# Layer 3's first steps issued between the steps that follow the recurrent part's last scan

## The chip, the cores and the metric

The kernel runs on one core of one Trainium2 chip. The metric is device time of one execution in microseconds (us). A core has a matrix engine (TensorE, PE in the profile, with its weight loads as PEld), a vector engine (VectorE, DVE), a scalar engine (ScalarE, ACT), a general engine (GpSimd, POOL) and a synchronisation engine (SyncE, SP), which here only issues loads and stores. Each engine works through its own list of instructions in the order in which they were written into it; engines wait for each other by semaphores. Matrix products land in PSUM (8 banks, a tile of 128 x 512 float32 fills one), everything else lives in SBUF.

## The reference, cut to what matters

Four layers follow each other on an activation x of shape (4, 512, 512) in float32, with a context tensor of the same shape.

```
# layer 0: grouped-query cross attention of x on the context, then layer norm
# layers 1 and 2: an RWKV block; x is its only link to the layer before
def step(s, inp):                     # one time step, for all batches and heads
    k_l, v_l, w_l, r_l = inp
    a = k_l[..., :, None] * v_l[..., None, :]
    out = einsum('bhs,bhst->bht', r_l, faaaa * a + s)
    return a + w_l[..., None] * s, out
_, outs = scan(step, s0, (k, v, w, r))
y = group_norm(outs) * gn_w + gn_b
x = x + (y * g) @ Wo.T                # "outputs"
xc = layer_norm(x)
xk2, xr2 = xc + shift(xc) * fmaa_k, xc + shift(xc) * fmaa_r
x = x + sigmoid(xr2 @ fWr.T) * (square(relu(xk2 @ fWk.T)) @ fWv.T)   # "channels"
# layer 3: queries from x, keys and values from [context, x], a mask over the context
q = x @ q_w + q_b
k, v = split(concat([ctx, x]) @ kv_w + kv_b)
attn = softmax(where(mask, q k^T / 32, -inf))        # 16 heads of 32, 1024 keys
o = (attn v) @ out_w + out_b + x
out = gelu(rmsnorm(o) @ mlp_w1 + b1) @ mlp_w2 + b2 + x
```

Batches do not mix anywhere: layer 3 on batch 0 needs only batch 0 of layer 2's result.

## The kernel before, in words

The residual x lies in SBUF for the whole run (`xn[b][lt]`, 16 tiles of 128 x 512). Four 8 KB slots per partition (`wpool`, tag `w`) hold whatever 512 x 512 weight is in use.

Layer 0 runs first (to about 730 us). Layers 1 and 2 are one function, `recurrent` (L455): its 16 units are (layer, batch, half of 256 positions), in this order. A global counter `g` runs through 8 scan steps per unit; `end` is 128. At each `g`, `summed` (L881), `begun` (L833 to L844), `scan` (L862, L867) and `repeated` are called, and then the dictionary `steps` says which parts of the other generators are due, in four phases EARLY, SOON, MID, LATE. These are `mixes` (the projections ahead of the scan), `outputs` (group norm, gate, output product; from step 9 of its unit) and `channels` (the feed-forward part; from step 19 to step 27 of its unit). So the last scan, at `g` = 127, is followed by 28 more values of `g` in which there is no scan left, but

* at g = 128 to 131 the end of the channels of unit 13 (products fk, fr, fv at L73 from g = 128, 129 and 130),
* at 129 to 135 the outputs of unit 15: mean, square, variance, a power on POOL (L929), a broadcast product pbc, the scaling, and the product with Wo,
* at 131 to 139 the channels of unit 14,
* at 139 to 147 the channels of unit 15, which need the outputs of unit 15.

Layer 3 is the function `layer3` (L1087). It opens its pools, loads its constants (L1100 to L1110), and for batch 0 loads the context and the mask (`begin`, L1117 to L1126), turns x by 16 transposes into `xT` (L1131, L1132) and makes query, keys and values of a first group of four heads (`prep`, L1143 to L1159). Then a loop over steps `i` starts, 8 of them (NB) for each of the 16 (batch, head group) pairs. At step `i` it calls `least` for the present group (four score products `psc`, L1175, into four PSUM tiles, and four DVE instructions L1189 that keep the row's smallest value, which is the largest score since the query is negated), one piece of the next group's `prep`, and, for the group before, `spread` (L1208), `turned` (L1175 pst, L1220), `weights` and `values`. In the first 8 steps there is no group before, so only `least` and `prep` run.

The order of instructions on PE, DVE, ACT and POOL is the order of the source (`manual_schedule`). SP's queue, which issues the loads, is laid out by the compiler's planner instead: it sends a load when, by the planner's clock, its buffer is free. SP issues in order, and a load whose buffer is still in use holds up those behind it. The loads with accumulation (`added`, L584) are issued from POOL.

Pools are stacks of memory: a pool that opens where another has closed gets its space, and a tile of it waits until the last user of the tiles that lay there is done. Before, all tiles of the recurrent part lie in `rm`, `rs`, `rpv` (4 banks), `rpy` (1 bank) and `rpp` (3 banks), and these close after g = 155; layer 3's pools open on the same space:

```
with tc.manual_schedule(engines={E.PE, E.DVE, E.Activation, E.Pool}):   # second block
    layer3()
```

Of the kernel before, what the change touches and what calls it, by code (L numbers as in the profile page):

```python
# [30 lines left out]
def tile_xattn_rwkv_perceiver(ctx: ExitStack, tc: tile.TileContext, t: dict, out: bass.AP):  # L31
# [422 lines left out]

    def recurrent(lp, ep):  # L455
        NI = 4
# [6 lines left out]

        mp = sp = pvr = pyp = W = A = None

# [89 lines left out]
        def scaled(tag, tiles, nm, rstd):  # L555
            if mp:
                z = mp.tile([P, NT, C], F32, tag=tag, name="z", bufs=BUFS[tag])
            else:
                z = wpool.tile([P, 2, NT, C], F32, tag="w", name="z0")[:, 0]
            for i, x in enumerate(tiles):  # L560
                nc.scalar.activation(
                    z[:, i], x, AF.Identity, bias=nm[:, i : i + 1], scale=rstd[:, i : i + 1]
                )
            return z
# [28 lines left out]
        def mixes(q):  # L593
# [83 lines left out]
            def product(x):  # L677
                dst = d[x] = mp.tile(full, F32, tag="o_" + x, name="o_" + x, bufs=1 if x == "v" else 2)
                dst4 = dst.rearrange("p i (o m) -> p i o m", o=2)
# [117 lines left out]
            yield 0, LATE  # L797
            y = d["y"] = mp.tile(full, F32, tag="y", name="y")
            nc.gpsimd.tensor_tensor(y, d["v"], al[:, None, :].to_broadcast(full), ALU.mult)
# [96 lines left out]
        def outputs(q):  # L896
# [8 lines left out]
            mm(pm, [(gmean, y[:, i, :]) for i in range(NI)])  # L905
            mean = sp.tile([P, TS], F32, tag="mean", name="mean", bufs=1)
            nc.scalar.copy(mean, pm)
            yield 9, LATE
            nc.vector.tensor_tensor(y, y, mean[:, None, :].to_broadcast(full), ALU.subtract)
            yield 10, EARLY  # L910
            sq = mp.tile(full, F32, tag="cx", name="sq", bufs=BUFS["cx"])
            nc.scalar.activation(sq, y, AF.Square)
            yield 10, SOON
            var = psum_tile([P, NQ], "var")
            for i in range(NI):
                for a in range(4):
                    nc.tensor.matmul(
                        var[32 * a : 32 * a + 32],
                        gm32,
                        sq[:, i, NQ * a : NQ * a + NQ],  # L920
                        start=(i == 0),
                        stop=(i == NI - 1),
                        tile_position=(0, 32 * a),
                    )
            yield 10, LATE
            rstd = sp.tile([P, NQ], F32, tag="gn_rs", name="gn_rs")
            nc.vector.tensor_scalar(rstd, var, 1.0, 1e-5, ALU.mult, ALU.add)  # L927
# [8 lines left out]
            mm(pm, [(gself, rp)])  # L936
            bc = sp.tile([P, TS], F32, tag="mean", name="bc", bufs=1)
            nc.scalar.copy(bc, pm)
# [3 lines left out]

            yg = mp.tile(full, F32, tag="cx", name="yg", bufs=BUFS["cx"])
            for i in range(NI):
# [24 lines left out]
        def channels(q):  # L969
# [8 lines left out]
            yield 22, EARLY  # L978
            cur = mp.tile([P, KC, TS], F32, tag="xc", name="xc", bufs=1)
            turned(z, vec, cur, V_LN2W, V_LN2B)  # L980
            last = d["lastc"] = sp.tile([P, KC], F32, tag="lastc", name="lastc")
            nc.scalar.copy(last, cur[:, :, TS - 1])
            yield 22, MID
            sx = mp.tile([P, KC, TS], F32, tag="sxc", name="sxc", bufs=1)
            shift(sx, cur, stT[:, :, b, 0] if hf == 0 else st[q - 1]["lastc"])

            def shifted(name, i):
                dst = mp.tile([P, KC, TS], F32, tag="cx", name=name, bufs=BUFS["cx"])
                for k in range(KC):
                    nc.scalar.activation(dst[:, k], sx[:, k], AF.Copy, scale=vec[:, k, i : i + 1])  # L990
                added(dst, cur)
                return dst
# [6 lines left out]

            kk = mp.tile([P, KC, TS], F32, tag="cx", name="kk", bufs=BUFS["cx"])  # L1000
            fk = load_w(t[n + "fWk"], n + "fk")
# [52 lines left out]
        end = G * len(units)  # L1054
        with (
            tc.tile_pool(name="rm", bufs=2) as mp,
            tc.tile_pool(name="rs", bufs=2) as sp,
            tc.tile_pool(name="rpv", bufs=1, space=PSUM) as pvr,
            tc.tile_pool(name="rpy", bufs=1, space=PSUM) as pyp,
            tc.tile_pool(name="rpp", bufs=3, space=PSUM) as pp,  # L1060
        ):
            psum["p"] = pp, "p"


            W = [mp.tile([P, 8, TP + 1], F32, tag=f"W{i}", name=f"W{i}", bufs=1) for i in range(2)]
            A = mp.tile([P, 8, TP + 1], F32, tag="A", name="A", bufs=1)
            for z in (*W, A):
                nc.gpsimd.memset(z[:, :, 0:1], 0.0)
            for g in range(at[0], end + 28):
                if 0 < g <= end:  # L1070
                    summed(g - 1)
                if -1 <= g < end - 1:
                    begun(g + 1)
                if 0 <= g < end:
                    scan(g)
                if 0 < g < end - 2 and g % NI == NI - 2:
                    repeated(*place(g + 2)[:2])
                for ph in (EARLY, SOON, MID, LATE):
                    for q, gen in steps.pop((g, ph), ()):
                        at = next(gen, None)  # L1080
                        if at:
                            follow(q, at, gen)
                    if ph == MID and 0 < g <= end and g % NI == 0:
                        taken(g - 1)


    def layer3():  # L1087
# [3 lines left out]
        T2 = 2 * P  # L1091
        with (
            tc.tile_pool(name="l3c", bufs=1) as cp,
            tc.tile_pool(name="l3b", bufs=1) as bp,
            tc.tile_pool(name="l3s", bufs=2) as sp,
            tc.tile_pool(name="l3ps", bufs=7, space=PSUM) as ps_s,
            tc.tile_pool(name="l3po", bufs=1, space=PSUM) as ps_o,
        ):
            cols = cp.tile([P, KC, 3], F32, name="cols3")
# [13 lines left out]
            def begin(b):  # L1113
# [3 lines left out]
                nc.sync.dma_start(cT, t["ctxT"][:, b * L : (b + 1) * L].rearrange("(k p) n -> p k n", p=P))  # L1117
                mi = sp.tile([P, L], I32, tag="sc", name="mi")
                nc.sync.dma_start(mi, t["mask3"][b : b + 1, :].to_broadcast([P, L]))
# [59 lines left out]
            def least(u, lt, a):  # L1179
# [3 lines left out]
                if (lt, a) == (0, 0):  # L1183
                    d["mx", m] = sp.tile([P, 2, LT, NR], F32, tag="mx", name="mx", bufs=2)
                mx = d["mx", m]
                ps = row_scores(d["q", m][:, lt * P : (lt + 1) * P], d["k", m][:, a, :], "psc")
                for r in range(NR):
                    sc = sp.tile([P, L], F32, tag="sc", name="sc", bufs=2)
                    nc.vector.tensor_tensor_reduce(  # L1189
# [10 lines left out]
            def spread(u):  # L1200

                b, m = u
                d = st[b]
                mb = d["mb"] = sp.tile([P, NR, L], F32, tag="mb", name="mb", bufs=1)
                for r in range(NR):
# [57 lines left out]
            def inverted(u):  # L1263
                d = st[u[0]]
                rs = d["rs"] = sp.tile([P, L], F32, tag="sc", name="rs")
                nc.vector.reciprocal(rs, d["pn"])
# [8 lines left out]
            def finish(b):  # L1275
# [5 lines left out]
                for lt in range(LT):  # L1281
# [5 lines left out]
                    nc.vector.tensor_tensor(ao, ao, x, ALU.add)  # L1287
                    sq = sp.tile([P, C], F32, tag="sc", name="sq")
                    ss = sp.tile([P, 1], F32, tag="ss", name="ss")
# [6 lines left out]
                for h in range(L // T2):  # L1296
                    nT = bp.tile([P, KC, T2], F32, tag="nT", name="nT", bufs=2)
                    for k in range(0, KC, 2):
# [16 lines left out]
                for h in range(L // T2):  # L1315
                    nT = nTs[h]
                    for j in range(4):
                        m1 = load_w(t["L3_W1"][:, j * C : (j + 1) * C], f"l3_m1_{j}")
                        hT = bp.tile([P, KC, T2], F32, tag="hT", name="hT", bufs=2)
                        for m in range(0, KC, 2):  # L1320
# [38 lines left out]
            LAG = 2  # L1359
            for _ in chain(begin(0), prep(0, 0)):  # L1360
                pass
            early = rest = iter(())
            left = 0
            for i in range(NU + NB + LAG):
                n, s = divmod(i, NB)
                u, old = [units[j] if 0 <= j < len(units) else None for j in (n, n - 1)]
                if u and s == 0:
# [17 lines left out]
                elif piece(rest):  # L1385
                    left -= 1
                if old:
                    if s == 0:
# [20 lines left out]
    E = mybir.EngineType  # L1409
    with (  # L1410
        tc.manual_schedule(engines={E.PE, E.DVE, E.Activation, E.Pool}),
        tc.tile_pool(name="rl", bufs=1) as lp,
        tc.tile_pool(name="rt", bufs=2) as ep,
    ):
        ahead = recurrent(lp, ep)
        layer0(ahead, ep)
        for _ in ahead:
            pass
    with tc.manual_schedule(engines={E.PE, E.DVE, E.Activation, E.Pool}):
        layer3()  # L1420

# [63 lines left out]
```

## Time and profile before

| | |
|---|---|
| median of 3 runs | 3794.02 us (3792.13 to 3795.58) |
| profiled execution | 3798.02 us, its span 3796.2 us, granted TensorE clock 0.966 |
| busy share of the span | PE 94%, DVE 73%, ACT 44%, POOL 47% |

By stage, in us (cut at the first layer-1 product, the last scan, layer 3's first projection, and the first step of layer 3 that works on two groups):

| stage | length | PE busy | DVE busy | ACT busy | POOL busy | granted clock |
|---|---|---|---|---|---|---|
| layer 0, 0 to 730 | 730 | 708.5 | 543.5 | 481.9 | 500.7 | 0.98 |
| 730 to 2290, recurrent part with scans | 1560 | 1425.5 | 1354.2 | 673.0 | 699.8 | 0.96 |
| 2290 to 2426.6, what follows the last scan | 136.6 | 93.1 | 19.0 | 34.7 | 33.4 | 0.84 |
| 2426.6 to 2479.2, layer 3's first group alone | 52.6 | 52.5 | 23.8 | 4.1 | 0 | 0.92 |
| 2479.2 to the end | 1317.0 | 1290.8 | 819.5 | 474.4 | 537.0 | 0.98 |

A row of the timeline begins with its start and its length in us, then the engine, the line, the operation, and the output and input by the program's names; what stands in brackets is how long the engine was idle before it and who released it. Matrix products are pipelined: the time from one row's start to the next row's start is what one costs in a stream, and it is a little less than the length shown.

### The profile page before, as it was taken

The page shows a single profiled execution, that of the slowest core. Times are in us where ns is not written, and L with a number is a line of the kernel's source. Part 1 is how long each engine was busy: PE and PEld are TensorE (multiplying, and loading weights), DVE is VectorE, ACT ScalarE, POOL GpSimd, SP SyncE. Part 2 cuts the span into 40 slices and gives each one's busy share as a digit, 9 for nine tenths or more (in the row PEclk, how much of TensorE's full clock was granted, in tenths as well). Part 3 has the DMA queues.
Part 4 walks back from the last instruction along what each step waited for, and adds up shares of the span by engine and source line. Part 5 has one row for each costly group of instructions (what it writes and reads, how often), then busy time and mean ns, then how long its engine had stood idle before and what let it go on. Part 6 is the DMA issues. An engine that isn't in the chain of part 4 may idle for free.

```text
span 3796.2 us, 52369 instructions
## 1 busy us (share of the span) xinstructions
PE 3570.5 (94%) x20544; PEld 1900.4 (50%) x20544; DVE 2759.9 (73%) x4665; ACT 1668.2 (44%) x2486; POOL 1771.0 (47%) x834
## 2 busy tenths in 40 slices
PE   9999999988899999999999977799999999999989
PEld 3333333455565666655655544444455445544446
DVE  6777777689988888888888882177866766667531
ACT  4777675533444444444444432133334434434421
POOL 4777876524544444444444443045533433344330
PEclk9999999989999999999999988899999999999999
DMA  4000000156676777777777764400022122121223
GB/s 151 24 12 23 12 9 20 40 141 141 146 171 165 170 188 177 170 173 179 163 171 167 169 156 111 111 28 19 15 76 83 56 70 95 56 73 34 95 95 122
DMA packets 188805, 386.66 MB, mean 102 GB/s; under 512 B 18128, under 2 KB 44880, under 8 KB 186512
## 3 DMA queue, kind: packets, MB, share of 16 engines
q1 hardware_dynamic: 150256, 251.72, 20.9%
q0 software_dynamic: 38304, 131.61, 18.7%
q8 instruction: 162, 2.65, 0.3%
q14 instruction: 83, 0.68, 0.1%
HBM read 247.50 MB, written 4.19 MB: 66 GB/s over the span
## 4 chain that ended last, share of the span: by engine, by line
PE 71%; DVE 13%; DMA 6%; issue 4%; POOL 3%; ACT 2%; SPq 0%; DVEq 0%; POOLq 0%; ACTq 0%
PE pm L73 9%; PE ph L73 6%; PE pv L73 6%; PE po L73 6%; DMA kv<-A 5%; PE psc L242 5%; PE pst L279 4%; PE pst L1175 4%; PE psc L1175 4%; PE pr L73 3%; PE pk L73 3%; PE po L304 3%; PE po L1241 3%; DVE ry L867 3%; DVE kv L862 2%
## 5 line engine op out<-in xcount | busy, mean ns | idle before, releaser
L1236 POOL TENSOR_TENSOR acc<-acc,aT 128x2048 f32<-128x2048 f32 x96 | 436.2, 4544 | 337.5 <-ACT aT L1231 220.0
L292 POOL TENSOR_TENSOR aT<-aT,nmT 128x1536 f32<-128x1536 f32 x124 | 428.7, 3461 | 205.5 <-ACT aT L290 182.2
L254 DVE CUSTOM_DVE_ANT_0 sc<-psc,nm 128x512 f32<-128x512 f32 x512 | 354.1, 692 | 147.2 <-PE psc L242 89.5
L1220 DVE TENSOR_TENSOR aT<-pst,mb 128x512 f32<-128x512 f32 x512 | 317.7, 683 | 166.0 <-PE pst L1175 166.0
L867 DVE TENSOR_TENSOR ry<-kv,o_r 128x1024 f32<-128x1024 f32 x256 | 347.4, 1398 | 3.5
L584 POOL DMA_DIRECT2D kv<-A x127 | 118.8, 936 | 381.4 <-DVE kv L839 378.3
L862 DVE TENSOR_TENSOR_SCAN kv<-W,kv 128x1032 f32<-128x1032 f32 x128 | 296.3, 2315 | 0.2 <-DMA kv<-A 0.2
L290 ACT COPY aT<-pst 128x512 f32<-128x512 f32 x372 | 196.5, 595 | 177.9 <-PE pst L279 177.4
L298 ACT ACTIVATE aT<-aT 128x2048 f32<-128x2048 f32 x128 | 246.7, 1929 | 5.4 <-POOL aT L292 4.6
L73 PE MATMUL ph<-nT,l_m 128*128 128x256 f32 x1024 | 238.1, 388 | 0.0
L73 PE MATMUL po<-l_m,hT 128*128 128x512 f32 x512 | 233.1, 602 | 0.0
L73 PEld LDWEIGHTS ph<-nT,l_m 128*128 128x128 f32 x1024 | 193.6, 193 | 64.1 <-issue 24.8
L833 DVE TENSOR_TENSOR A<-vr,o_k 128x1024 f32<-128x1024 f32 x128 | 155.7, 1217 | 87.9 <-DMA kv<-A 87.8
L279 PE MATMUL pst<-q,km 32*128 32x512 f32 x1024 | 206.5, 640 | 9.4 <-DVE mxs L254 5.8
L1234 POOL TENSOR_TENSOR acc<-aT 128x2048 f32<-128x2048 f32 x16 | 72.4, 4527 | 303.2 <-ACT aT L1229 303.2
L1189 DVE CUSTOM_DVE_ANT_0 sc<-psc,zeros,mx 128x512 f32<-128x512 f32 x256 | 176.6, 746 | 51.2 <-PE psc L1175 49.0
L1231 ACT ACTIVATE aT<-aT 128x2048 f32<-128x2048 f32 x64 | 122.3, 1911 | 191.8 <-DVE aT L1220 191.6
L1229 ACT ACTIVATE aT<-aT,mc 128x2048 f32<-128x2048 f32 x64 | 128.1, 2002 | 165.1 <-DVE aT L1220 158.9
L242 PE MATMUL psc<-km,q 32*128 32x512 f32 x1024 | 198.5, 651 | 0.8 <-ACT q L223 0.8
L929 POOL TENSOR_TENSOR gn_rs<-gn_rs,mhalf 128x64 f32<-128x64 f32 x16 | 186.4, 11648 | 23.1 <-DVE gn_rs L927 23.1
L881 PE MATMUL py<-ry,k 128*32 128x512 f32 x1024 | 159.6, 637 | 39.1 <-DVE ry L867 27.6
L1189 DVE CUSTOM_DVE_ANT_0 sc<-psc,nm 128x512 f32<-128x512 f32 x256 | 161.1, 686 | 39.2 <-PE psc L1175 39.2
(265 smaller groups left out, 7153.3 us busy)
## 6 DMA issues: line engine op xcount, KB each, us to landing
l_m<-in_L_W SPq DMA_DIRECT2D x64, 1024.0 KB, 5.1
kv<-A POOLq DMA_DIRECT2D x127, 516.0 KB, 7.4
L_wk<-in_L_Wk SPq DMA_DIRECT2D x16, 1024.0 KB, 8.0
L_wr<-in_L_Wr SPq DMA_DIRECT2D x16, 1024.0 KB, 7.7
L_wv<-in_L_Wv SPq DMA_DIRECT2D x16, 1024.0 KB, 5.9
L_wg<-in_L_Wg SPq DMA_DIRECT2D x16, 1024.0 KB, 8.0
L_wo<-in_L_Wo SPq DMA_DIRECT2D x64, 256.0 KB, 7.6
L_fk<-in_L_fWk SPq DMA_DIRECT2D x16, 1024.0 KB, 7.8
```

The source lines that it names most:

```text
L73: nc.tensor.matmul(ps, lhsT, rhs, start=(i == 0), stop=(i == len(pairs) - 1))
L242: nc.tensor.matmul(psc, d["q"][g][rs, lt * P : (lt + 1) * P], d["km"][rs, a, :], start=True, stop=True, tile_position=(32 * r, 0),)
L254: nc.vector.tensor_tensor_reduce(sc, ps[r], d["nm"][lt], 1.0, -3.0e38, ALU.add, ALU.max, mxs[:, a, lt, c : c + 1])
L279: nc.tensor.matmul(pst, d["km"][rs, a, s * P : (s + 1) * P], d["q2", a][rs, :], start=True, stop=True, tile_position=(32 * r, 0),)
L292: nc.gpsimd.tensor_tensor(w[:, n:, :], w[:, n:, :], nmT[:, None, :].to_broadcast([P, NR - n, L]), ALU.add)
L298: nc.scalar.activation(w, w, AF.Exp)
L862: nc.vector.tensor_tensor_scan(flat(kv), flat(W[g % 2]), flat(kv), 0.0, ALU.mult, ALU.add)
L867: nc.vector.tensor_tensor(y, kv[:, 4 * h : 4 * h + 4, None, :TP].to_broadcast([P, 4, 2, TP]), d["r"][:, i].rearrange("p (o m) -> p o m", o ...
L1175: nc.tensor.matmul(psc, lhsT[rs], rhs[rs], start=True, stop=True, tile_position=(32 * r, 0))
L1189: nc.vector.tensor_tensor_reduce(sc, ps[r], d["nm"][a], 1.0, mx[:, 0, lt, r : r + 1] if a else 3.0e38, ALU.add, ALU.min, mx[:, a, lt, r : ...
L1220: nc.vector.tensor_tensor(w[:, r, :], ps[r], d["mb"][:, r, :], ALU.subtract)
L1236: nc.gpsimd.tensor_tensor(d["acc", m], d["acc", m], w, ALU.add)
```

## The change

It does four things.

1. The recurrent part's pools are split. Tiles that are still used after the last scan (the gate `o_g`, `y`, everything with tag `cx`, `xc`, `sxc`, `mean`, `gn_rs`, `lastc`) move to new pools `rq` and `rt2`; they and the 3 banks of `rpp` are opened first. The rest (`rm`, `rs`, `rpv`, `rpy`) is opened on top and closed at g = 128. Names, sizes and numbers of buffers stay as they are (`sq` as a tile name becomes `y2`).
2. Layer 3's `cp` and `bp` are opened on the other end of SBUF, and a first PSUM pool of 5 banks (`l3pf`), where `rpv` and `rpy` were. The tiles that the first steps need (`mi`, `sc`, `mx`, `mb`, and with them `rs` and `sq` of tag `sc`) go to `bp`; `nT` and `hT` go from `bp` to `l3s`. `l3s`, the 7 banks of `l3ps` and the one of `l3po` are opened after the recurrent part's pools are closed.
3. `layer3` becomes a generator. It yields at each point where `begin` and `prep` yield (2 and 5 times) and after each of the first 8 steps `i` (8 times), then "closed". `recurrent` takes one such piece after the LATE phase of each g from 129 on, so the 15 pieces stand at g = 129 to 143, and the one that closes `l3pf` at 144. The pieces are: constants, loads of batch 0 and half of the transposes; the other half; q; k of the context; v of the context; k of x; v of x; then five times `least` with a piece of the next group's `prep` (q, k, v, k, v), and three times `least` alone.
4. There is one `manual_schedule` block instead of two.

```diff
-        with (
-            tc.tile_pool(name="rm", bufs=2) as mp,
-            tc.tile_pool(name="rs", bufs=2) as sp,
-            tc.tile_pool(name="rpv", bufs=1, space=PSUM) as pvr,
-            tc.tile_pool(name="rpy", bufs=1, space=PSUM) as pyp,
-            tc.tile_pool(name="rpp", bufs=3, space=PSUM) as pp,
-        ):
+        with ExitStack() as below, ExitStack() as above:
+            mq = below.enter_context(tc.tile_pool(name="rq", bufs=2))
+            sq = below.enter_context(tc.tile_pool(name="rt2", bufs=2))
+            pp = below.enter_context(tc.tile_pool(name="rpp", bufs=3, space=PSUM))
+            mp = above.enter_context(tc.tile_pool(name="rm", bufs=2))
+            sp = above.enter_context(tc.tile_pool(name="rs", bufs=2))
+            pvr = above.enter_context(tc.tile_pool(name="rpv", bufs=1, space=PSUM))
+            pyp = above.enter_context(tc.tile_pool(name="rpy", bufs=1, space=PSUM))
...
+                if g == end:
+                    above.close()
+                elif g > end:
+                    next(beside, None)
+            for _ in beside:
+                pass
...
     def layer3():
...
-            tc.tile_pool(name="l3c", bufs=1) as cp,
-            tc.tile_pool(name="l3b", bufs=1) as bp,
-            tc.tile_pool(name="l3s", bufs=2) as sp,
-            tc.tile_pool(name="l3ps", bufs=7, space=PSUM) as ps_s,
-            tc.tile_pool(name="l3po", bufs=1, space=PSUM) as ps_o,
+            cp = opened("l3c", 1, side="right")
+            bp = opened("l3b", 1, side="right")
+            first = ExitStack()
+            ps_s = first.enter_context(tc.tile_pool(name="l3pf", bufs=5, space=PSUM))
...
-            for _ in chain(begin(0), prep(0, 0)):
-                pass
+            yield from chain(begin(0), prep(0, 0))
...
             for i in range(NU + NB + LAG):
                 n, s = divmod(i, NB)
+                if i == NB:
+                    first.close()
+                    yield "closed"
+                    sp = opened("l3s", 2)
+                    ps_s = opened("l3ps", 7, space=PSUM)
+                    ps_o = opened("l3po", 1, space=PSUM)
...
+                if i < NB:
+                    yield
...
-        ahead = recurrent(lp, ep)
+        third = layer3()
+        ahead = recurrent(lp, ep, iter(third.__next__, "closed"))
         layer0(ahead, ep)
         for _ in ahead:
             pass
-    with tc.manual_schedule(engines={E.PE, E.DVE, E.Activation, E.Pool}):
-        layer3()
+        both.close()
+        for _ in third:
+            pass
```

## The prediction

> **What bounds the kernel now.** I read the stages first (busy time of each engine by window). Their columns are the window, its length, then busy time and instructions of PE, PEld, DVE, ACT and POOL, the granted clock, the DMA share and GB/s.
>
> ```profile
> 2290.00:2426.60 136.60, 93.11 (x305) 52.68 (x303) 19.00 (x32) 34.70 (x71) 33.40 (x26) 0.84 0.52 139
> 2426.60:2479.20 52.60, 52.54 (x248) 30.03 (x248) 23.82 (x69) 4.12 (x6) 0.00 (x0) 0.92 0.13 35
> ```
>
> In the 137 us after the last scan no engine is full: PE rests for 43 us. In the next 53 us layer 3's first group runs alone. Everywhere else PE is at 90% or more. So the change has about 190 us to work on. The timeline of PE there says what it waits for:
>
> ```profile
> 2301.04 8.83 PE L73 MATMUL pm<-xk,L_fk 128*128 128x256 f32 x32 [3.19 <-DMA xk<-xc]
> ...
> 2311.44 7.03 PE L73 MATMUL pr<-L_fr,xr 128*128 128x512 f32 x16
> 2320.10 0.65 PE L917 MATMUL var<-sq,gm 128*32 128x64 f32 x32 [1.63 <-ACT sq L912]
> 2320.68 7.13 PE L73 MATMUL pv<-L_fv,kk 128*128 128x512 f32 x16
> 2332.79 1.22 PE L73 MATMUL pbc<-rp,gsel 128*128 128x256 f32 x2 [4.97 <-ACT rp L933]
> 2333.81 2.29 PE L572 MATMUL ptn<-ident,z 128*128 128x128 f32 x8
> 2341.90 8.92 PE L73 MATMUL pm<-L_wo,yg 128*128 128x512 f32 x16 [5.80 <-POOL yg L952]
> 2350.71 7.15 PE L73 MATMUL pm<-xk,L_fk 128*128 128x256 f32 x32
> ...
> 2376.31 0.47 PE L572 MATMUL ptn<-ident,z 128*128 128x128 f32 x1 [4.72 <-ACT z L561]
> ...
> 2388.96 9.29 PE L73 MATMUL pm<-xk,L_fk 128*128 128x256 f32 x32 [10.18 <-DMA xk<-xc]
> 2398.09 7.03 PE L73 MATMUL pr<-L_fr,xr 128*128 128x512 f32 x16
> 2404.95 7.03 PE L73 MATMUL pv<-L_fv,kk 128*128 128x512 f32 x16
> 2412.84 1.97 PE L1131 MATMUL ptx<-ident,x 128*128 128x128 f32 x16 [0.85 <-DVE xr L1029]
> 2426.66 5.75 PE L73 MATMUL pq<-xT,w3q 128*128 128x512 f32 x8 [11.86 <-DMA w3q<-in_L_Wq]
> 2432.25 3.60 PE L73 MATMUL pk<-cT,w3k 128*128 128x512 f32 x8
> ```
>
> The gaps (3.2, 1.6, 5.0, 5.8, 4.7, 10.2, 0.9, 11.9) are one chain of small steps through ACT, POOL and DMA. The last is the way into layer 3, which the chain of waits shows: layer 3's loads wait for a buffer that the last accumulating DMA still reads.
>
> ```profile
> 2413.07 5.38 DMA x<-xr
> 2420.08 6.45 DMA w3q<-in_L_Wq
> 2426.66 5.75 PE pq L73 x8
> ```
>
> **The change, part by part.** I call a product by its weight and unit (fk13 is the fk product of unit 13) and count from fk13 at 2301.04, which stays, to layer 3's first `spread` (pb), which starts at 2484.16.
>
> *Moved PE work* (start to start in a stream): 16 transposes 1.9, a q or k product 3.43 (2432.25 to 2435.68), a v product 3.6, four psc 1.07. With the second group's projections: 1.9 + 6 x 3.43 + 4 x 3.6 + 8 x 1.07 = 45.4 us. It takes 2412.84 to 2477.24 = 64.4 us now; the rest is the 11.9 us wait, a cold start (pq 5.75 against 3.60) and a stretch where the minima on DVE set the pace (32 psc matmuls in 9.1 us instead of 4.3).
>
> *Moved loads.* SP issues constants, context, mask and three weights, 2.8 MB, in about 7 us. They need the scan's space, free when the last py ends (2297.85), and stand behind Wo15 (issued by 2299.6). With Wo15 (1 MB) and the accumulations xk, xr (0.5 MB each) that is 4.8 MB; at the 184 GB/s of the window 2350 to 2370 it is through 26 us after 2297, at 2323, the mask (some 4 MB ahead) at 2319. First needs: nm and mc on DVE, which stand ahead of gn_rs, due there at 2321.9; q's weights at 2329.6. So nothing is paid, with 3 and 7 us to spare. xr13 is issued at 2297.2; an accumulation under load took 11.2 us (at 2214.09), so it lands by 2308.4, before fr13. Later weights (fk14 at 2309.9, needed at 2360) have tens of us. POOL's memsets (0.5 and 0.9) fall into its 23 us of rest ahead of the power.
>
> *The tail with its pieces*, each engine in order, durations from the rows:
> - g = 129, 130: fr13 ends at 2318.3, 8 transposes to 2319.2. ACT's two copies (0.5 each) push the square to 2320.1, var to 2321.2, so gn_rs and the power (10.6) end at 2332.9 instead of 2331.7. fv13 and 8 transposes to 2329.6.
> - g = 131 to 133: q to 2333.1, k to 2336.5. On ACT, z14 stands behind the k eviction (2337.4) and so runs to 2338.9 instead of 2334.3: this is the price of order, 4.6 us, and the broadcast factor to 2339.2, y scaled (DVE) to 2340.5. v to 2340.7.
> - g = 134, 135: transposes to 2341.7, xc and yg on ACT to 2345.5, gate on POOL to 2347.9, sxc to 2350.0. k of x to 2345.1, so Wo15 waits 2.9 us and starts at 2348.0. A rest of 3.19 us cost fk13 8.83 - 7.15 = 1.7 us, the nearest row, so 6.9 + 1.7: 2356.6. v of x to 2360.2.
> - g = 136 to 138: xk14 is there at 2356.9 (sxc to product took 6.9 at 2382.02 to 2388.96), so fk14, fr14, fv14 (7.0, 6.9, 6.9) and three pieces (4.7, 4.7, 4.8) run without a gap, to 2395.2.
> - g = 139 to 143: behind piece 10's v (DVE to 2395.9), xr and statistics end at 2399.2, rstd at 2400.3; z15 to 2401.8. Five PSUM banks hold one `least` and one projection, so psc now waits for DVE's minima (2.5 to 2.7 a step): turned15 ends at 2408.3, sxc15 at 2412.1, the last psc at 2413.2.
> - g = 144 to 147: fk15 at 2412.1 + 6.9 = 2419.0, cold, 9.1; fr15, fv15 6.9 each: 2441.9. Then psc of step 8 (one bank waits for the last xr: 2443.2), q, and pb at 2446.7.
>
> The sum: 2484.2 - 2446.7 = 37.5, taken as 37 us. From step 8 on nothing is changed but places, and PE is busy 1290.8 of 1317 us there, so it only starts earlier.
>
> [...]
>
> *Split pools, one block.* The trace shows no cost of a pool's place. At layer 0's end the recurrent part's first product (pmm at 730.72) waits 1.05 us for DVE to empty a PSUM bank; in other banks that wait can go or double, 1.05 us either way. I take 0, between them.
>
> *Bounds of the overlap.* Least: nothing overlaps, PE does tail and pieces one after the other: fv15 at 2411.9 + 45.4 = 2457.3 against 2477.2 before step 8, a gain of 20 (the wait for loads and the slow minima still go). Most: the gaps at Wo15 (2.9) and fk15 (5.8 and its cold 2.1) vanish too: 47. I take 37, which goes by the rows step by step, where each bound denies or grants them all; the case runs from 27, about halfway to the lower bound, to 47.
>
> **The rivals.**
> - *Loads late.* The planner lays out SP; if it puts layer 3's loads behind fv14's (issued at 2327.85 now), the mask lands about 10 us later (4.2 to issue, 5.6 to land, as at 2418.6 to 2424.69), DVE stands still before gn_rs until 2338, and power, pbc and all after are 16 us later: gain 21. Against it: their space is free at 2297.85, before fk14's slot (2309.9). For it: the planner goes by its own clock, which no row shows. 3794 - 21 = 3773.
> - *No overlap*, the bound above: gain 20, 3774. It needs every piece to hold up its step by its full length; the gaps of 5 to 10 us behind POOL and DMA speak against it.
> - *Slower: the scan loop is stretched.* All its tiles and banks lie elsewhere now. Scans start from 778.4 to 2286.5, 11.87 us apart, with DVE busy 1323 of 1510 us, so a delay there isn't absorbed. The place is DVE's product into A, which waits 87.8 us in all for the accumulating DMA kv<-A. From 37 / 127 = 0.29 us a step on, the gain is gone; at 0.4 the time is 3794 - 37 + 51 = 3808. Against it: nothing in the loop's order, sizes or buffers changes.
>
> A queue that stands still is a smaller danger than it looks:
>
> ```profile
> SPq L728 <- PE pp L73: 113.3, 1, 113.3
> ```
>
> SP once stood 113 us behind a load whose space was not free, but a layer-3 load waits for the scan alone, so only the tail's weights can be behind it, and those have time.
>
> **How the numbers follow.** The sum is against the profiled execution, 3798.0 (span 3796.2 and 1.8 around it): 3761.0. It lies 4.0 above the median, so the forecast is 3794.0 - 37 = 3757. Chances: the forecast (27 to 47, so 3747 to 3767) 0.70; loads late 0.12; no overlap 0.08; stretched loop 0.07; about nothing 0.03. Forecast and late loads make 0.82, so the range is 3747 to 3775. About 0.2% (7.6 us) is what a measurement can tell from no change: faster 0.90, same 0.03, slower 0.07.
>
> **What would show it.** Right: psc rows between fk14, fr14 and fv14; PE's rest from 2298 to the first pb falling from over 43 us to under 20, with the longest gaps before Wo15 and fk15; the power ending 1 to 2 us later; pb about 145 us after fk13's start instead of 183; the scans still 11.87 us apart. Wrong: DVE idle behind the mask's DMA ahead of gn_rs (late loads); pb 160 us or more after fk13 with PE full (no overlap); scans further apart (stretched loop).

## The result

| | median | runs |
|---|---|---|
| before | 3794.80 us | 4 runs, 3792.13 to 3797.16 |
| after | 3754.99 us | 4 runs, 3747.64 to 3761.29 |

The ratio is 0.9886, 95% interval 0.9868 to 0.9905: 40 us less. The forecast was 3757, with 3747 to 3775 as its range. The same kernel run once more, beside its own runs of the kernel before (called `again` below), gave 3746.07 against 3793.81, ratio 0.9871 (0.9854 to 0.9889). The profiled execution took 3749.93 us, its span was 3748.2 us and its granted clock 0.971 (before: 3798.02, 3796.2, 0.966).

### The profile after

In this profile fk13 starts at 2293.56, 7.48 us earlier than in the profile of before, so a clock time of the prediction less 7.48 is the time to look for. The busy time by window comes first, with the same columns as in the prediction. The two stretches that the prediction began with, moved by 7.48, and then the stretch that the prediction counted, from fk13 to the first `spread` (pb):

```profile
2282.52:2419.12 136.60, 121.30 (x512) 72.22 (x510) 39.89 (x97) 36.19 (x74) 30.69 (x24) 0.95 0.49 126
2419.12:2471.72 52.60, 51.75 (x255) 25.23 (x254) 28.95 (x67) 15.09 (x16) 15.33 (x5) 1.00 0.30 86
2293.56:2438.04 144.48, 133.50 (x538) 77.74 (x539) 38.22 (x102) 35.08 (x69) 27.55 (x20) 0.96 0.51 136
```

The counted stretch before:

```profile
2301.04:2484.16 183.12, 142.75 (x539) 82.03 (x540) 38.79 (x102) 35.53 (x69) 28.14 (x22) 0.85 0.40 109
```

The last row of after and this one hold the same work (539 and 538 matmul records) and differ by 38.6 us. PE's rest in the stretch falls from 183.12 - 142.75 = 40.4 us to 144.48 - 133.50 = 11.0, which is 29.4 us. The other 9.2 us are busy time: at a granted clock of 0.96 rather than 0.85 the same products are shorter. So a fourth of the gain is not rest that was filled, but the lower clock at which products ran behind those rests (before, from start to start of the next: 0.79 in Wo15 behind 5.80 us, 0.76 in fk15 behind 10.18, 0.63 in pq behind 11.86).

PE's timeline after, with the columns as before:

```profile
2293.56 9.09 PE L73 MATMUL pm<-xk,L_fk 128*128 128x256 f32 x32 [5.18 <-DMA xk<-xc]
...
2304.22 7.03 PE L73 MATMUL pr<-L_fr,xr 128*128 128x512 f32 x16
2311.08 1.04 PE L1142 MATMUL ptx<-ident,x 128*128 128x128 f32 x8
2313.85 0.65 PE L917 MATMUL var<-y,gm 128*32 128x64 f32 x32 [1.73 <-ACT y L912]
...
2329.15 0.59 PE L73 MATMUL pbc<-rp,gsel 128*128 128x256 f32 x2
...
2333.15 1.04 PE L572 MATMUL ptn<-ident,z 128*128 128x128 f32 x8
2334.02 3.60 PE L73 MATMUL pk<-xT,w3k 128*128 128x512 f32 x8
2340.43 7.13 PE L73 MATMUL pm<-L_wo,yg 128*128 128x512 f32 x16 [2.81 <-POOL yg L952]
...
2350.97 7.07 PE L73 MATMUL pm<-xk,L_fk 128*128 128x256 f32 x32
2357.97 1.14 PE L1186 MATMUL psc<-kT,q 32*128 32x512 f32 x8
...
2409.91 8.95 PE L73 MATMUL pm<-xk,L_fk 128*128 128x256 f32 x32 [5.59 <-issue]
...
2433.43 1.14 PE L1186 MATMUL psc<-kT,q 32*128 32x512 f32 x8 [0.85 <-DVE xr L1029]
...
2438.04 1.91 PE L1219 MATMUL pb<-ident,mx 128*128 128x128 f32 x16
```

Of the gaps of before, 1.7 us at var, 2.8 at Wo15, 5.6 at fk15 and 0.9 are left. The waits at pbc (5.0), at z15's transposes (4.7) and at layer 3's weights (11.9) are gone. The chain that ended last shows what the longest one left consists of: POOL's shift, ACT's scaling of xk, and then the accumulating DMA xk<-xc, which POOL issued at 2405.24. The chain doesn't name that DMA; it shows ACT's scaling of xr and "issue" in its place (in `split`, below, the same wait stands as `<-DMA xk<-xc`):

```profile
2401.16 1.88 POOL sxc L588
...
2403.26 0.39 issue
2403.65 1.29 ACT xk L990 x3
2404.94 1.60 ACT xr L990 x4
2406.55 3.36 issue
2409.91 8.95 PE pm L73 x32
```

SP's queue, and DVE's rows that need the first of these loads:

```profile
2287.42 0.33 SPq L956 DMA_DIRECT2D L_wo<-in_L_Wo  x1
2288.55 0.37 SPq L1111 DMA_DIRECT2D cols<-in_L_cols  x1
...
2300.01 1.37 SPq L1154 DMA_DIRECT2D w3v<-in_L_Wv  x1
2301.43 2.79 SPq L956 DMA_DIRECT2D L_wo<-in_L_Wo  x3
```

```profile
2306.03 0.42 DVE L1132 TENSOR_SCALAR nm<-mi 128x512 f32<-128x512 int32 x1
...
2314.57 0.23 DVE L927 TENSOR_SCALAR gn_rs<-var 128x64 f32<-128x64 f32 x1 [8.04 <-PE var L917]
```

Layer 3's eleven loads go out between the first quarter of Wo15 and the other three, over 12.8 us. The mask is in SBUF when DVE comes to it, and DVE rests 8 us more before it has work for gn_rs.

Outside the counted stretch, the profiles differ by 7.5 us up to fk13 and by 1.8 us behind pb (1312.0 and 1310.2 us). Whether those 7.5 us belong to the change is one of the questions below.

### The profile page after: what moved, and what is told of

The parts are those of the page before. It is cut to its first block, busy times and chain, and to the rows that moved or that the text cites. A ratio compares the mean times of both kernels' runs of the same rounds, so it can differ in the third digit from the quotient of the medians.

```text
span 3748.2 us, 52355 instructions
## 1 busy us (share of the span) xinstructions
PE 3561.1 (95%) x20544; PEld 1894.1 (51%) x20544; DVE 2748.8 (73%) x4665; ACT 1667.2 (44%) x2486; POOL 1762.1 (47%) x834
## 4 chain that ended last, share of the span: by engine, by line
PE 72%; DVE 12%; DMA 5%; issue 4%; POOL 3%; ACT 3%; SPq 0%; POOLq 0%; DVEq 0%; ACTq 0%
PE pm L73 10%; PE ph L73 6%; PE pv L73 6%; PE po L73 6%; DMA kv<-A 5%; PE psc L242 5%; PE pst L279 5%; PE pst L1186 4%; PE psc L1186 4%; PE po L1252 3%; PE po L304 3%; PE pr L73 3%; PE pk L73 3%; DVE ry L867 3%; DVE kv L862 2%
## 5 line engine op out<-in xcount | busy, mean ns | idle before, releaser
L254 DVE CUSTOM_DVE_ANT_0 sc<-psc,nm 128x512 f32<-128x512 f32 x512 | 354.1, 692 | 147.0 <-PE psc L242 89.3
L1186 PE MATMUL psc<-kT,q 32*128 32x512 f32 x1024 | 171.0, 646 | 12.3 <-DVE aT L1231 11.5
```

Source lines behind the costliest of these rows:

```text
L254: nc.vector.tensor_tensor_reduce(sc, ps[r], d["nm"][lt], 1.0, -3.0e38, ALU.add, ALU.max, mxs[:, a, lt, c : c + 1])
L1186: nc.tensor.matmul(psc, lhsT[rs], rhs[rs], start=True, stop=True, tile_position=(32 * r, 0))
```

## The experiments

"fk13 to pb" is the length of the counted stretch in the profiled execution of each kernel; "scans" is the time from the start of the first scan to that of the last. Ratios are against the kernel before, run on the same chip.

| kernel | what it is | fk13 to pb | scans | median, us | ratio (95%) |
|---|---|---|---|---|---|
| before | | 183.1 | 1508.2 | 3794.80 | |
| before2 | before once more | 184.7 | 1490.8 | 3785.97 (one run) | |
| banks | before, PSUM pools in the new order | 182.7 | 1497.0 | 3791.34 | 1.0007 (0.9996 to 1.0019) |
| places | before, SBUF pools split, none closed early | 183.9 | 1488.7 | 3789.02 | 0.9999 (0.9988 to 1.0009) |
| left | all of the change but the pieces and the other end of SBUF | 186.2 | 1490.6 | 3793.61 | 1.0010 (0.9997 to 1.0023) |
| split | all of the change but the pieces | 169.8 | 1501.5 | 3774.26 | 0.9942 (0.9923 to 0.9961) |
| behind | all pieces after the last step | 169.6 | 1489.0 | 3770.04 | 0.9939 (0.9921 to 0.9957) |
| prep | only the first 7 pieces between the steps | 158.7 | 1494.5 | 3760.13 | 0.9919 (0.9899 to 0.9940) |
| after | | 144.5 | 1495.3 | 3754.99 | 0.9886 (0.9868 to 0.9905) |
| again | after once more | 146.7 | 1493.1 | 3746.07 | 0.9871 (0.9854 to 0.9889) |
| held | pieces of the second group's projections from step 3 on | 140.5 | 1492.3 | 3741.58 | 0.9860 (0.9839 to 0.9881) |
| held2 | held once more | 141.3 | 1497.5 | 3746.08 | 0.9886 (0.9871 to 0.9901) |
| later | held, no piece at g = 132 | 147.0 | 1494.3 | 3756.00 | 0.9911 (0.9897 to 0.9926) |
| two | held, two pieces at g = 134, none at 135 | 140.6 | 1490.3 | 3743.35 | 0.9876 (0.9846 to 0.9905) |

The theory was the prediction's: the pieces fill PE's rest, loads are hidden, and the pools' places and the single block change nothing by themselves. Its rival was that the places do something: the scan loop was 12.9 us shorter in the profile after (1495.3 against 1508.2).

### The kernel after once more

> The changed kernel once more, for its spread. Theory 'overlap': the gain is what layer 3's pieces do in PE's rests behind the last scan (38.6 us from fk13 to the first pb in the first profile), and the scan loop's length is chance: about 3756, ratio 0.988 to 0.992, and the time from first to last scan lies somewhere between 1495 and 1510 us. Rival 'places': the scan loop is shorter for good, because its tiles lie elsewhere now (1495.3 us from first to last scan in the first profile, against 1508.1 before): again 1495, give or take 3, and a ratio of 0.987.

Measured: 146.7 us from fk13 to pb, 1493.1 for the scans. In this profile Wo15 took 8.83 us after the same rest of 2.81 us after which it took 7.13 in the first profile; that is 1.7 of the 2.2 us between the two. The loop is again shorter than in the first profile of before.

### The pools split and in one block, but no pieces between the steps

```diff
-                elif g > end:
-                    next(beside, None)
-            for _ in beside:
-                pass
```

Layer 3 is then issued as a whole behind the recurrent part, as before, but its tiles lie where the scan's lay.

> Only the pools are split and put elsewhere, and there is one block of order; layer 3 starts behind the closed pools as before. Theory 'overlap': no change, ratio 0.998 to 1.002, from fk13 to the first pb 183 us. Rival 'places': the shorter loop alone, 3795 - 13 = 3782, ratio 0.9966.

Measured: 169.8 us and a ratio of 0.9942. The first theory, by which this kernel would be as slow as before, falls: nothing of layer 3's computation has moved, and yet the stretch is 14 us shorter than in the kernels that leave it as it was (183.6, the mean of before, before2, banks and places). The timeline says where, here from `split`, the last products of unit 15 and the first of layer 3:

```profile
2385.91 9.19 PE L73 MATMUL pm<-xk,L_fk 128*128 128x256 f32 x32 [10.10 <-DMA xk<-xc]
...
2409.68 1.97 PE L1138 MATMUL ptx<-ident,x 128*128 128x128 f32 x16 [0.85 <-DVE xr L1029]
2411.48 3.60 PE L73 MATMUL pq<-xT,w3q 128*128 128x512 f32 x8
```

The gaps of the recurrent part's end stand as before (10.10 ahead of fk15), but pq follows the transposes at once and takes 3.60 us. Before, it waited 11.86 us for its weights and took 5.75: 11.9 + 2.1 = 14.0. The loads are no longer late, because the space that they need is free behind the last scan: SP sends them among the tail's weights, this one 28 us behind fk13's start, although the product that uses it comes 86 us later:

```profile
2325.84 0.51 SPq L1150 DMA_DIRECT2D w3q<-in_L_Wq  x1
```

### All pieces behind the last step

```diff
-                elif g > end:
-                    next(beside, None)
```

The loop `for _ in beside` stays, so the pieces are issued behind g = 155 and ahead of the closing of the recurrent part's other pools.

> All fifteen pieces are issued behind the last step of the recurrent part, but before its pools close, so that layer 3's loads go out early and nothing overlaps on the engines. Theory 'overlap': the wait for the loads (11.9 us) and the cold start behind it (2.2) go, nothing else: 3795 - 14 = 3781, ratio 0.9963; 169 us from fk13 to pb. Rival 'places': 14 + 13 = 27 us less, 3768, ratio 0.993.

Measured: 169.6 us, the same as `split`. Whether layer 3's first work is issued before or after the closing of the pools is of no matter; what brings the 14 us is in both kernels.

### The first 7 pieces alone between the steps

```diff
-                elif g > end:
+                elif end < g <= end + 7:
```

> Only the first seven pieces (loads, transposes, first group's projections) stand between the steps; the eight steps with minima follow behind the tail. By 'overlap' the seven pieces hide most of their 19 us and their waits: from fk13 to pb about 169.7 (early loads alone) less 15, 155 us; the eight steps hide the other 10. If the minima pieces do the hiding, 165 us or more.

Measured: 158.7 us, 3.7 over the 155 expected. Part of that is not the pieces: in this profile fk13 followed without a rest and took 7.17 us, where it took 8.66 to 9.76 behind a rest in all others but `behind`, so the stretch is some 1.5 to 2.6 us shorter by what lies ahead of it. As the stretches stand, the first seven pieces, 19.4 us of PE work by the prediction's prices (1.9 + 3 x 3.43 + 2 x 3.6), bring 169.7 - 158.7 = 11.0 us. The eight others, 26.0 us of PE work, bring 158.7 - 145.6 = 13.1 (145.6 is the mean of after and again). In `prep` the end of the tail looks as before again:

```profile
2369.03 0.48 PE L572 MATMUL ptn<-ident,z 128*128 128x128 f32 x1 [4.72 <-ACT z L561]
...
2381.59 9.23 PE L73 MATMUL pm<-xk,L_fk 128*128 128x256 f32 x32 [10.10 <-DMA xk<-xc]
...
2428.26 7.89 PE L1186 MATMUL psc<-kT,q 32*128 32x512 f32 x24
2437.38 2.09 PE L1186 MATMUL psc<-kT,q 32*128 32x512 f32 x8 [1.23 <-DVE mx L1200]
2439.40 5.89 PE L73 MATMUL pq<-xT,w3q 128*128 128x512 f32 x8
```

The gaps of 4.72 and 10.10 are there, and so is the stretch where the score products wait for DVE's minima, with a cold q behind it (5.89 against 3.70).

### Before once more, and with the new places alone

`before2` is the kernel before without an edit.

> The kernel before once more, for a second profile of its scan loop (1508.1 us from first to last scan in the first one; 1489 to 1501.5 in five profiles of kernels with split pools). If the loop's length is chance, some value between 1490 and 1510; if the places of the tiles set it, 1505 to 1511.

`banks` opens the PSUM pool of 3 banks first, so that every tile of the recurrent part lies in the bank that it has after the change:

```diff
         with (
+            tc.tile_pool(name="rpp", bufs=3, space=PSUM) as pp,
             tc.tile_pool(name="rm", bufs=2) as mp,
             tc.tile_pool(name="rs", bufs=2) as sp,
             tc.tile_pool(name="rpv", bufs=1, space=PSUM) as pvr,
             tc.tile_pool(name="rpy", bufs=1, space=PSUM) as pyp,
-            tc.tile_pool(name="rpp", bufs=3, space=PSUM) as pp,
         ):
```

> The kernel before with one thing of the change: the three PSUM banks of the recurrent part's products are opened ahead of the scan's five, so that both lie in other banks. If the banks make the loop shorter: about 3785, ratio 0.9975, loop about 1495. If not: ratio 0.9985 to 1.0015, loop about 1508.

`places` takes the split of the SBUF pools alone; all close behind the last step, as before:

```diff
+            tc.tile_pool(name="rq", bufs=2) as mq,
+            tc.tile_pool(name="rt2", bufs=2) as sq,
             tc.tile_pool(name="rm", bufs=2) as mp,
...
-            y = d["y"] = mp.tile(full, F32, tag="y", name="y")
+            y = d["y"] = mq.tile(full, F32, tag="y", name="y")
```

> The kernel before with another thing of the change: the SBUF pools of the recurrent part are split, so that the scan's tiles lie elsewhere, but all pools close after the tail, banks and layer 3 stay. If the places in SBUF make the loop shorter: about 3785, ratio 0.9975, loop about 1495. If not: ratio 0.9985 to 1.0015, loop about 1508. Layer 3's loads are late as before in both cases: about 183 us from fk13 to pb.

Measured: ratios of 1.0007 and 0.9999, both with intervals that hold 1, and 182.7 and 183.9 us from fk13 to pb. The loop without any edit took 1490.8 us in `before2`, as short as in any changed kernel, and 1508.2 in the first profile. The loop's length is thus not a matter of the change: from one execution to the next it differs by up to 20 us over the fourteen profiles (1488.7 to 1508.2), and the first profile of before was the longest of all. The rival falls, and so does the reading that the change made fk13 start 7.5 us sooner: those are 12.9 us in the loop, less 4.4 by which the first scan started later and 1.0 more between the last scan and fk13. Where the loop was long, DVE waited longer for the accumulating DMA of the scan:

```profile
DVE A L833 <- DMA kv<-A: 87.8, 38, 5.9
```

```profile
DVE A L833 <- DMA kv<-A: 70.3, 38, 5.9
```

The first row is from the first profile of before, the second from `before2`: 87.8 and 70.3 us in all, 38 waits each. The 17.5 us between them are as much as the loops differ by (17.4), although over the other profiles the two don't go so closely together.

### Which part of `split` does it

`left` is `split` with layer 3's pools on the end of SBUF where they were before:

```diff
-            cp = opened("l3c", 1, side="right")
-            bp = opened("l3b", 1, side="right")
+            cp = opened("l3c", 1)
+            bp = opened("l3b", 1)
```

> As split (nothing of layer 3 issued between the steps, one block), but layer 3's pools cp and bp on the same end of SBUF as the recurrent part's, so that they lie where the tables and the tail's tiles lay. Placement makes split's gain of 13 us: the loads wait again for the tail's last users, pq waits 10 to 13 us after fv15, fk13 to pb 182 to 185 us, time as before (ratio 0.998 to 1.002). One block makes it: pq right behind fv15, fk13 to pb 168 to 171 us, ratio 0.994 to 0.996.

Measured: 186.2 us, ratio 1.0010, and the wait is back:

```profile
2413.71 5.92 PE L73 MATMUL pq<-xT,w3q 128*128 128x512 f32 x8 [11.59 <-DMA w3q<-in_L_Wq]
```

SP issues this load only at 2407.22, 119 us behind fk13's start and not 28 as in `split`:

```profile
2407.22 0.79 SPq L1150 DMA_DIRECT2D w3q<-in_L_Wq  x1
```

So it is the place of layer 3's tiles that brings the 14 us. The single block and the split of the recurrent part's pools, which `left` has too, bring nothing by themselves.

### Where the pieces stand

In the profile after, fk15 still waits 5.6 us, while the five steps with a piece of the second group's projections stand early, between products of unit 14 that need nothing in between. `held` moves these projections three steps later:

```diff
-                if piece(early):
+                if i > 2 and piece(early):
```

> The second group's five projections are taken with the steps i = 3 to 7 of layer 3 instead of 0 to 4, so that the minima run on DVE beside the products fk14, fr14 and fv14 and the projections fill PE between z15 and fk15. Theory 'overlap': PE no longer waits for PSUM banks at g = 140 to 143 (about 4 us) and the rest before fk15 shrinks from 5.6 to about 2 us; pb comes 9 us earlier, 136 us behind fk13 instead of 144.5: 3746, ratio to before 0.987 or what 'again' has minus 0.0024. Rival 'places': as 'again'.

Measured: 140.5 us, and 141.3 when run again beside the next kernel:

> The kernel with the first three steps bare once more, beside the next one. Pieces as a way to fill gaps: fk13 to pb 140 to 141 us, the gap ahead of fk15 2.5 us, the median 8 to 14 us below the after kernel's 3746 to 3755 if the prior profile was typical, 3738 to 3748. If the gain over the after kernel was chance: 3746 to 3755.

That is 5 us less than the 145.6 of the change, where 136 was expected; about 1 us of the 5 is that Wo15 ran cold in `again` (8.83 us) and in neither of these two (7.13). The rest ahead of fk15 is 2.53 to 2.54 us rather than 5.6, but fk15 isn't any shorter (8.83): in `two`, below, where it took 8.83 behind the same 2.54 us, the granted clock read 0.50 from 2398.00 to 2400.40; this is what the expectation missed in part. The medians (3741.58 and 3746.08, against 3754.99 and 3746.07 for the change) point the same way, but their runs overlap, so that the gain is shown by two profiles of each kernel, not by the times.

`later` tests the price of order that the prediction gave as 4.6 us, that z14 stands behind the key's eviction on ACT:

```diff
-                elif g > end:
+                elif g > end and g != end + 4:
```

> As held2, but no piece at g = 132, so the key product of the context and its eviction on ACT stand one step later and z14 is not behind it. The price of order (4.6 us in the prediction, the eviction was 3.4 us in the way in the trace): z14 starts on ACT about 3 us earlier relative to fk13, and the gap ahead of Wo15 is 0 to 1 us instead of 2.8; PE waits instead some 2 us for the broadcast factor after q. If the order sets the end of the tail: fk13 to pb 137 to 139 us. If PE is the bound there and only exchanges one gap for another: 140 to 142 us, and the median is that of held2.

Measured: 147.0 us, 5.7 more than `held2`; neither case that was expected. In `held2` (first fence) and in `later` (second):

```profile
2342.01 7.13 PE L73 MATMUL pm<-L_wo,yg 128*128 128x512 f32 x16 [2.80 <-POOL yg L952]
```

```profile
2324.89 0.70 PE L73 MATMUL pbc<-rp,gsel 128*128 128x256 f32 x2 [1.66 <-ACT rp L933]
...
2336.27 8.83 PE L73 MATMUL pm<-L_wo,yg 128*128 128x512 f32 x16 [2.81 <-POOL yg L952]
...
2381.72 3.29 PE L1186 MATMUL psc<-kT,q 32*128 32x512 f32 x6 [2.57 <-DVE mx L1200]
2384.94 5.05 PE L73 MATMUL pq<-xT,w3q 128*128 128x512 f32 x8
```

z14 did start 2.3 us sooner on ACT, counted from fk13, and Wo15 1.4 us sooner (46.0 against 47.4), but PE now waits 1.66 us at pbc, and the rest ahead of Wo15 is the same 2.81. Behind it every piece stands a step later, and this costs more than was won: Wo15 ran cold (1.7 us), two steps of minima come so close that PE waits 2.57 us for DVE, q behind that wait is cold too (5.05 against 3.70), and the last score and value products (4.7 us) fall between fk15 and fr15. With the eviction out of its way z14 thus won Wo15 1.4 us, not the 4.6 of the prediction.

That the rest ahead of Wo15 was 2.8 us in all six profiles led to the last kernel. From z14's transposes to the end of the gate it is a chain of 7.3 us (2334.74 to 2342.01 in `held2`; 7.26 to 7.41 in all six), beside which PE has one product. `two` puts the value product of x there as well:

```diff
-                elif g > end:
-                    next(beside, None)
+                elif g > end and g != end + 7:
+                    next(beside, None)
+                    if g == end + 6:
+                        next(beside, None)
```

> As held2, but the value product of x is issued at g = 134, right behind the key product of x and ahead of Wo15, and nothing at g = 135. If the gap ahead of Wo15 (2.79 to 2.81 us in every profile of these kernels) is only what the chain from z14's transposes to the gate, 7.3 us long, leaves beside one product: Wo15 starts without a gap, some 0.8 us later behind the transposes than in held2, and fk14, which then stands right behind Wo15, waits 1 to 2 us for xk14, which the trace of held2 lets land about 8.5 us after Wo15's start; fk13 to pb 140 us, 1 to 1.5 us below held2 (141.3, less where Wo15 ran cold). If something else holds Wo15 (z14 behind the eviction on ACT), the gap stays and v delays all behind it: 143 to 145 us. The median cannot tell 1 us.

```profile
2326.24 3.60 PE L73 MATMUL pk<-xT,w3k 128*128 128x512 f32 x8
2329.67 3.73 PE L73 MATMUL pv<-w3v,xT 128*128 128x128 f32 x32
2333.24 7.03 PE L73 MATMUL pm<-L_wo,yg 128*128 128x512 f32 x16
2341.51 7.14 PE L73 MATMUL pm<-xk,L_fk 128*128 128x256 f32 x32 [1.23 <-DMA xk<-xc]
```

Wo15 starts without a rest, fk14 waits 1.23 us, both as expected. The stretch is 140.6 us, but in this profile fv13 took 8.83 us instead of the 7.13 that it took in all the others (behind the same 1.73 us of rest and the small var products); without that it would be 138.9. The median, 3743.35 us, does not tell it from `held`.

## Why the prediction was right

**The time and its sum.** 37 us were forecast; the medians fell by 40 and, in `again`, by 48, the counted stretch by 38.6. That the median came within 2 us of the forecast is partly luck, since the two medians of the changed kernel differ by 9 us (3754.99 and 3746.07); the stretch is the better measure. Over all profiles that leave this stretch as it was (the five first rows of the table, mean 184.1) and the two of the change (145.6) it is 38.5: 14.4 by the place of the tiles (to 169.7), 11.0 by the first seven pieces, 13.1 by the other eight (the last two less sure by the 2 us of fk13 in `prep`).

**Step by step.** In the clock of the profile of before (the rows above plus 7.48; predicted in brackets): fr13 2311.7 (2311.4), var 2321.3 (2321.2), pbc 2336.6 (2336.5), Wo15 2347.9 (2348.0) after 2.81 us of rest (2.9), fk14 2358.5 (2360.2), fk15 2417.4 (2419.0) after 5.59 (5.8), pb 2445.5 (2446.7). The order of the engines, worked out row by row, held to within 0.3 us up to Wo15. Its largest mis-sized term is there: Wo15 was put at 8.6 us, by fk13's cold start behind 3.19 us, and took 6.97 from start to start. That alone is 1.6 us, while pb came 1.2 us sooner, so all the other terms together were 0.4 us too low. With Wo15 at 6.9 us the sum would give a gain of 39, which is what this profile shows, but by chance: in `again`, Wo15 was cold (8.67 us from start to start), and there the sum as it stood was right within about 1 us: 183.1 - 146.7 = 36.4.

**The loads.** Hidden, as predicted, but by another order. They were taken to stand behind Wo15 on SP's queue and to go out in 7 us; they went ahead of three of Wo15's quarters and took 12.8 us, and those quarters, 12 us later than they were, still had 36 us to their product. DVE came to the mask without a wait. The rival "loads late" falls on these rows. That fk13 itself waited 5.18 us for its accumulation rather than 3.19 isn't owed to them: with the loads in the same place `again` waited 3.23, and `before2`, without them, 4.56.

**The lower bound.** "No overlap" was priced at 20 us, as the case in which the wait for the loads and the slow minima go and nothing else does. `behind` is that case, and it gives 14: with nothing in between, the minima still follow each other and still hold up PE (6.94 us for 24 score products, 2.18 us of wait and a cold q of 5.16):

```profile
2434.83 6.94 PE L1184 MATMUL psc<-kT,q 32*128 32x512 f32 x24
2443.95 2.09 PE L1184 MATMUL psc<-kT,q 32*128 32x512 f32 x8 [2.18 <-DVE mx L1198]
```

The minima's share of the 20 was wrong; it goes only when the steps are spread out. The mechanism, loads that are early because of where their tiles lie, was in the working (the wait of 11.9 and the cold start). The upper bound was added up too low: 37 + 2.9 + 5.8 + 2.1 is 47.8, not 47, and Wo15's cold 1.7 would go with its rest (in `two`, without a rest, Wo15 took 7.03). The forecast does not rest on it.

**Split pools and one block.** Taken as 0, with 1.05 us either way. `left`, `banks` and `places` agree: ratios of 0.9999 to 1.0010, all with 1 in their interval. That holds for the recurrent part's pools and the block; the place of layer 3's pools is worth 14 us by itself, which the prediction has only inside the gain of the whole, and the expectation of `split` had at nothing. The "stretched loop" falls too: with the change the loop took 1493.1 to 1495.3 us, without it 1488.7 to 1508.2.

**The signs named beforehand.** PE's rest from the last py to the first pb was to fall below 20 us, and is 5.18 + 11.0 = 16.2; its longest gaps in the counted stretch are at Wo15 and fk15; pb comes 144.5 us behind fk13's start (145 was named). The power ended 1.2 us later (2332.9, in the clock of before, against 2331.7), and score products stand between fk14, fr14 and fv14. One sign was poorly chosen: "scans still 11.87 us apart" is a figure that one execution of the kernel before doesn't share with the next.

**What stays open.** `again` gained 48 us by its median, while its counted stretch explains 36 to 37, and `split` and `behind` 20 and 24, where theirs explain 14. Single runs of one kernel lie up to 12 us to either side of its median (once 18), and the loop alone differs by 20 us between profiles, so these 6 to 11 us may be chance. But the interval of `again`, 42 to 55 us, does not hold 37, and those of `split` and `behind`, from 15 and 16 us up, do not hold 14. These kernels and `held` (52 by its median and 44 by its stretch) share the same eleven runs of before, and in the batches run later the two figures lie closer (`prep` 29 and 25, `held2` 43 and 43, `later` 33 and 37, `two` 48 and 44). The profiles show no other place for a gain: behind pb it is 1312.0 to 1312.4 us in before, before2, banks and places, and 1310.2 and 1308.2 in after and again, 2 to 4 us less; fk13 starts at 2287.0 to 2301.0 us in the four and at 2288.8 to 2293.6 in the two. No run here settles it.

## What to carry to other kernels

Where work is moved forward, its loads and its computation are two gains, and the loads may need no move at all: here 14 of 38 us came from tiles laid on space that is free early, with the instructions where they had been. Where pieces are put into gaps, go through each engine's list row by row and keep the pieces for the gaps that are longest: work put between steps that have no gap only fills PE's list, and is missing later, where PE rests (here 145.6 us against 140.9, the mean of `held` and `held2`). And before a difference between two profiles is explained, the same kernel profiled twice tells how much of it is there without any change.

## What the runs showed of the hardware

A rest of PE that cost nothing in one execution cost 1.7 us in another. Behind the same 2.8 us of rest Wo15 took 7.13 us in three profiles (after, held, held2) and 8.73 to 8.83 in three others (again, prep, later). The windows around it show the granted clock, first after, then `again`: the rest, 1.6 us of Wo15, and the next 3.42.

```profile
2337.63:2340.43 2.80, 0.00 (x0) 0.00 (x1) 0.00 (x0) 0.89 (x2) 2.39 (x2) 1.00 0.32 94
2340.43:2342.03 1.60, 1.60 (x4) 0.87 (x5) 0.00 (x0) 0.00 (x0) 1.60 (x1) 1.00 0.00 0
2342.03:2345.45 3.42, 3.42 (x9) 1.52 (x8) 0.69 (x1) 3.03 (x8) 1.23 (x3) 1.00 0.00 0
```

```profile
2332.58:2335.38 2.80, 0.00 (x1) 0.00 (x1) 0.00 (x0) 0.89 (x2) 2.39 (x2) 1.00 0.31 94
2335.38:2336.98 1.60, 1.60 (x4) 0.77 (x5) 0.00 (x0) 0.00 (x0) 1.60 (x1) 0.89 0.00 0
2336.98:2340.40 3.42, 3.42 (x6) 1.45 (x5) 0.00 (x0) 3.03 (x8) 1.23 (x3) 0.55 0.00 0
```

In `again` the clock falls only when Wo15 has already begun; it stands at 0.89 and 0.55 in these two windows and at 1.00 again in the 1.60 us behind them. For the products fk, fv and Wo of the counted stretch, over all profiles: rests of 0.95 and 1.23 us, seen once each, cost nothing; 1.63 to 1.73 us, ahead of the small var products and fv13, cost nothing in all profiles but one, where fv13 took 8.83 (`two`, the granted clock at 0.50 from 2305.60 to 2308.00); 2.54 us cost 1.7 each of three times; 2.8 us cost it three times in six; and rests of 3.19 to 10.21 us cost at least 1.5 every time. What decides whether a rest between 1.6 and 2.8 us costs anything, no run here shows.
